# Spreading a softmax maximum with float32r matmuls instead of float32 ones, in a Perceiver kernel on one Trainium2 core

## The chip, the cores and the metric

The kernel runs on one core of a Trainium2 chip. A core has five engines that run side by side and meet only at semaphores: TensorE (PE, with its weight loads listed as PEld), VectorE (DVE), ScalarE (ACT), GpSimd (POOL) and SyncE (SP), which here issues all transfers. The metric is the device time of one execution in microseconds (us). Before the change it is 2708.26 us, the median of three runs that lie between 2706.93 and 2709.93 us.

## What is computed

The reference is a small Perceiver with six residual blocks, on an input `x` of 8 batches of 64 rows by 512 and a context of 8 batches of 1601 rows by 512. Each block is fed a layer-normalised `x`:

```
x = x + cross_attention_0(ln(x), ctx, Wq, bq, Wkv, bkv, Wo, bo)   # 32 query heads of 128, 8 key/value heads
x = x + state_space_block(ln(x), ...)                             # 1024 channels, 16 states, a scan over 64 steps
x = x + ternary_linear(ln(x), weight, bias)
x = x + cross_attention_1(ln(x), ctx)                             # no weights
x = x + causal_self_attention(ln(x), wq, wk, wv, wo)              # 32 heads of 16, rotary
x = x + octonion_ffn(ln(x), w_gate, w_up, w_down)
```

The change is in the first block, whose core is, for every batch and key/value head:

```
scores = einsum('blkgd,bmkd->bkglm', q, k) * scale
attn   = softmax(scores, axis=-1)          # over the 1601 context rows
o      = einsum('bkglm,bmkd->blkgd', attn, v)
out    = o @ Wo + bo
```

A softmax is unchanged when the same number is taken off all scores of a query, so the number taken off need not be the exact maximum, as long as it is the same in numerator and denominator.

## The kernel before

**Units.** The first attention is cut into 64 units, one for each batch `b` and key/value head `i`. A unit has 256 queries (four heads of 64 rows) and 1601 context rows, in 13 tiles of up to 128. Scores are held transposed: context rows on the 128 partitions, the 256 queries along the free axis. `x_k` (L354) makes keys, `x_v` (L319) values, `x_s` (L369) the scores, `x_av` (L454) the product with the values, `x_o` (L466) the normalisation, and `x_wo` (L496) the output projection. Keys, values and scores (and from batch 2 on the output projection) are made of three float32r products of a high and a low part (`split`, L100: ACT rounds the high part, DVE or POOL makes the low part); the product with the values and the sum over ones (L472) are plain float32.

**The maximum.** `x_s` keeps a running maximum `mx` on DVE (L390, L392, L395), which leaves a maximum for each partition and query. `x_max` (L397) turns it with two transposes on PE into `m_ps` (L403), and one DVE reduction (L405) writes the negative maximum of each query to the two columns of `mc`. `x_spread` (L408) puts that number on all partitions: for each half `h` of 128 queries a matmul (L412) has as stationary operand column `h` of `mc`, broadcast to 128 by 128, and as moving operand the identity; entry (p, j) of its result is the negative maximum of query j. `x_exp` (L416) then adds this to the score tiles `S` on DVE (L426), takes the exponential on ACT (L427) and sums on POOL (L429, L446, L448, L452).

**Order of the work.** `x_all` (L527) goes through the units in six steps each. While unit n makes its scores, unit n-1 goes through maximum, spread, exponential and value product, so that one unit of each kind is in flight. `x_spread` is emitted in step 0, after the unit's first score tiles. Beside this run side programs: `prep` (L616, splits of weights), and `chain` (L779), the five later blocks, for four groups of two batches. `advance` (L1331, in `run`) emits pieces of them after every piece of the first attention, by fixed costs (X_COST, PREP_COST, CHAIN_COST) that the change leaves alone. The fourth group's chain starts after the last unit, so its work and what is left of the third group's form the tail. The calls only give a first order: the tile framework's scheduler then puts the instructions of each engine in an order of its own, by times that it estimates. Only the DVE, ACT and POOL instructions of the side programs are kept in program order, while the first attention runs (`Late`, L55). So the price that the scheduler sees for one matmul can move others.

**Constants.** `consts` (L147) makes the identity `ident` on POOL (L152) at the start.

Of the kernel before, what the change touches and what calls it, by code (L numbers as in the profile page):

```python
# [9 lines left out]
FR = mybir.dt.float32r  # L10
# [6 lines left out]
P = 128  # L17
# [61 lines left out]
class Kernel:  # L79
# [67 lines left out]
    def consts(self):  # L147
        nc, i = self.nc, self.i
        c = self.ctx.enter_context(self.tc.tile_pool(name="const", bufs=1))
        self.c = c  # L150
        self.ident = c.tile([P, P], FP, name="ident")
        make_identity(nc, self.ident)  # L152
        self.eps5 = c.tile([P, 1], FP, name="eps5")
        nc.gpsimd.memset(self.eps5, 1e-5)
        self.ones = c.tile([P, P], FP, name="ones")
        nc.gpsimd.memset(self.ones, 1.0)
        self.eps6 = c.tile([P, 1], FP, name="eps6")
        nc.gpsimd.memset(self.eps6, 1e-6)

        def ld(name, shape):  # L160
            t = c.tile(shape, FP, name="c_" + name)
            nc.sync.dma_start(out=t, in_=i[name])
            return t

        self.bq = ld("bq", [P, 32])
        self.bk = ld("bk", [P, NKV])
        self.bv = ld("bv", [P, NKV])
# [229 lines left out]
    def x_max(self, b, i):  # L397

        nc = self.nc
        m = self.mf.pop((b, i))  # L400
        ps = self.px.tile([P, 2, 256], FP, name=self.nm("m_ps"), tag="m", bufs=MB)
        for h in range(2):
            nc.tensor.transpose(ps[:, 0, h * P : (h + 1) * P], m[:, 0, h * P : (h + 1) * P], self.ident)  # L403
        col = self.sb("mc", [P, 2], pool=self.xp, bufs=2)
        nc.vector.tensor_reduce(col, ps[:, 0].rearrange("p (h k) -> p h k", k=P), AX.X, ALU.max, negate=True)  # L405
        self.mm[(b, i)] = (ps, col)

    def x_spread(self, b, i):  # L408

        ps, col = self.mm[(b, i)]  # L410
        for h in range(2):
            self.nc.tensor.matmul(  # L412
                ps[:, 1, h * P : (h + 1) * P], lhsT=col[:, h : h + 1].to_broadcast([P, P]), rhs=self.ident, start=True, stop=True
            )

    def x_exp(self, b, i, n):  # L416
# [1086 lines left out]
```

## Time and profile before

| | |
|---|---|
| median of three runs | 2708.26 us |
| the profiled execution: own time / span of its instructions | 2710.54 / 2708.8 us |
| busy share of PE, PEld, DVE, ACT, POOL | 95, 84, 62, 50, 46 % |
| mean granted TensorE clock | 0.977 |
| last spread matmul (L412) ends | about 2384 us |
| spread matmuls (L412): records, mean of one | 256, 283 ns |
| DVE additions of the maximum (L426) | 448 |

The profile lists every matmul record with its own duration, from start to end; neighbours overlap, so the pace of a run of matmuls is read from start to start or from a run's length, not from one record's duration. A float32 matmul stands as two records, each with a weight load; a float32r matmul as one. The 64 units have two halves, so the 256 records of L412 are 128 matmuls. "Idle before" is the time in which the engine had nothing to run before an instruction, with the instruction that ended it. Lines such as L65 are helpers' lines through which the side programs are recorded.

### The profile page before, as it was taken

The page shows a single profiled execution, that of the slowest core. Times are in us where ns is not written, and L with a number is a line of the kernel's source. Part 1 is how long each engine was busy: PE and PEld are TensorE (multiplying, and loading weights), DVE is VectorE, ACT ScalarE, POOL GpSimd, SP SyncE. Part 2 cuts the span into 40 slices and gives each one's busy share as a digit, 9 for nine tenths or more (in the row PEclk, how much of TensorE's full clock was granted, in tenths as well). Part 3 has the DMA queues.
Part 4 walks back from the last instruction along what each step waited for, and adds up shares of the span by engine and source line. Part 5 has one row for each costly group of instructions (what it writes and reads, how often), then busy time and mean ns, then how long its engine had stood idle before and what let it go on. Part 6 is the DMA issues. An engine that isn't in the chain of part 4 may idle for free.

```text
span 2708.8 us, 43887 instructions
## 1 busy us (share of the span) xinstructions
PE 2569.9 (95%) x16288; PEld 2274.8 (84%) x16288; DVE 1670.9 (62%) x2723; ACT 1354.6 (50%) x3128; POOL 1253.5 (46%) x1243
## 2 busy tenths in 40 slices
PE   7999999999999899999999999999999999977787
PEld 6999999889899799978988988988898888964545
DVE  4444345577687865545577676554657777668744
ACT  4444554444566554544455545544546545446443
POOL 3212434464589864422358457521239556405410
PEclk9999999999999999999999999999999999987898
DMA  9544446665666235655234543665343454476764
GB/s 309 153 141 155 137 144 227 200 209 179 212 215 204 71 117 164 210 185 172 88 110 135 157 148 101 206 197 173 101 133 91 137 162 151 141 236 216 233 234 174
DMA packets 302934, 455.59 MB, mean 168 GB/s; under 512 B 80248, under 2 KB 179576, under 8 KB 298240
## 3 DMA queue, kind: packets, MB, share of 16 engines
q1 hardware_dynamic: 302720, 452.79, 52.2%
q8 instruction: 128, 2.10, 0.3%
q14 instruction: 86, 0.70, 0.1%
HBM read 380.23 MB, written 72.48 MB: 167 GB/s over the span
## 4 chain that ended last, share of the span: by engine, by line
PE 67%; DVE 10%; POOL 9%; DMA 7%; issue 4%; ACT 3%; SPq 0%; POOLq 0%; DVEq 0%; ACTq 0%
PE v_ps L334 15%; PE k_ps L363 15%; PE o_ps L464 10%; PE s_ps L385 8%; POOL a L65 4%; DVE a L65 3%; PE w_ps L521 3%; PE acc L274 3%; PE acc L819 2%; PE acc L1095 2%; POOL ss L452 2%; PE acc L1039 2%; PE acc L774 1%; PE acc L777 1%; DMA d_wo<-b 1%
## 5 line engine op out<-in xcount | busy, mean ns | idle before, releaser
L363 PE MATMUL k_ps<-cxb,wk 128*128 128x384 f32 x2304 | 469.9, 347 | 32.1 <-DVE mx L392 16.8
L334 PE MATMUL v_ps<-wv,cxb 128*128 128x256 f32 x3456 | 471.0, 283 | 1.4 <-DVE mx L392 1.2
L334 PEld LDWEIGHTS v_ps<-wv,cxb 128*128 128x128 f32 x3456 | 439.2, 189 | 22.0 <-issue 14.0
L363 PEld LDWEIGHTS k_ps<-cxb,wk 128*128 128x128 f32 x2304 | 405.2, 191 | 50.2 <-DVE mx L392 19.8
L464 PE MATMUL o_ps<-S,v 128*128 128x256 f32 (+1 forms) x1664 | 413.3, 381 | 6.0 <-DVE rw L479 3.9
L385 PE MATMUL s_ps<-q,kt 128*128 128x256 f32 (+1 forms) x2496 | 413.7, 299 | 5.2 <-DVE kt L109 3.1
L388 ACT COPY S<-s_ps 128x512 f32<-128x512 f32 (+1 forms) x448 | 242.4, 553 | 250.0 <-PE s_ps L385 246.9
L385 PEld LDWEIGHTS s_ps<-q,kt 128*128 128x128 f32 (+1 forms) x2496 | 342.1, 185 | 28.0 <-issue 6.9
L452 POOL TENSOR_TENSOR ss<-ss,S 128x512 f32<-128x512 f32 x254 | 353.7, 1392 | 14.6 <-ACT S L427 1.5
L429 POOL TENSOR_TENSOR ss<-S,S 128x512 f32<-128x512 f32 x64 | 85.0, 1328 | 586.9 <-ACT S L427 586.6
L392 DVE TENSOR_TENSOR mx<-s_ps,mx 128x512 f32<-128x512 f32 x256 | 175.4, 685 | 289.5 <-ACT S L388 288.8
L464 PEld LDWEIGHTS o_ps<-S,v 128*128 128x128 f32 (+1 forms) x1664 | 299.5, 190 | 45.0 <-issue 5.7
L108 ACT ACTIVATE kt<-k_ps,c_bk 128x384 fp32r<-128x384 f32 (+1 forms) x256 | 152.0, 594 | 240.7 <-PE k_ps L363 239.6
L426 DVE TENSOR_TENSOR S<-S,m_ps 128x512 f32<-128x512 f32 (+1 forms) x448 | 257.3, 641 | 24.4 <-PE m_ps L412 23.9
L427 ACT ACTIVATE S<-S 128x512 f32<-128x512 f32 (+1 forms) x448 | 247.4, 599 | 44.4 <-DVE S L426 43.8
L109 DVE SCALAR_TENSOR_TENSOR kt<-k_ps,c_bk,kt 128x384 fp32r<-128x384 f32 (+1 forms) x256 | 161.0, 629 | 170.9 <-ACT kt L108 169.4
L337 ACT COPY v<-v_ps 128x256 f32<-128x256 f32 (+1 forms) x416 | 152.7, 369 | 198.1 <-PE v_ps L334 195.7
L334 PE MATMUL v_ps<-wv,cxt 128*128 128x256 f32 (+1 forms) x1536 | 213.2, 286 | 2.7 <-DVE kt L109 1.6
L334 PEld LDWEIGHTS v_ps<-wv,cxt 128*128 128x128 f32 (+1 forms) x1536 | 195.3, 176 | 15.5 <-issue 6.5
L65 DVE TENSOR_TENSOR_SCAN a<-a,a 128x512 f32<-128x512 f32 x96 | 156.1, 1629 | 65.4 <-POOL a L65 65.4
L363 PE MATMUL k_ps<-cxt,wk 128*128 128x450 f32 x768 | 181.1, 378 | 0.9 <-DVE mx L392 0.8
L65 ACT ACTIVATE a<-lv,c_A_log 128x128 f32<-128x128 f32 x384 | 123.0, 394 | 105.3 <-DVE a L65 103.8
(358 smaller groups left out, 3971.3 us busy)
## 6 DMA issues: line engine op xcount, KB each, us to landing
wo<-d_wo SPq DMA_DIRECT2D x96, 512.0 KB, 5.0
wk<-d_wk SPq DMA_DIRECT2D x63, 512.0 KB, 3.8
wv<-d_wv SPq DMA_DIRECT2D x31, 1024.0 KB, 5.6
cst<-in_ctxT_dram SPq DMA_DIRECT2D x96, 192.0 KB, 3.1
b<-in_ctxN_dram SPq DMA_DIRECT2D x36, 512.0 KB, 3.9
d_q<-q_t SPq DMA_DIRECT2D x32, 512.0 KB, 4.4
q<-d_q SPq DMA_DIRECT2D x64, 256.0 KB, 3.5
d_wo<-b SPq DMA_DIRECT2D x32, 512.0 KB, 3.1
```

The costliest lines, as they stand in the source:

```text
L65: return lambda *a, **k: self.tc.keep_in_program_order(f(*a, **k))
L109: eng.scalar_tensor_tensor(lo, src, bias, hi.bitcast(FP), ALU.add, ALU.subtract)
L334: nc.tensor.matmul(ps[:r], lhsT=cx[:, a, c, o : o + r], rhs=w[:, m, c, :], start=k == 0, stop=k == 11)
L337: nc.scalar.copy(vt[:r], ps[:r])
L363: nc.tensor.matmul(ps[:, :wd], lhsT=w[:, a, c, :], rhs=cx[:, m, c, :], start=k == 0, stop=k == 11)
L385: nc.tensor.matmul(sp[:r, gi, :], lhsT=kt[:, a, o : o + r], rhs=q[:, m, :], start=k == 0, stop=k == 2)
L388: nc.scalar.copy(s[:r, :n], sp[:r, :n])
L392: nc.vector.tensor_tensor(mx, sp, S[0] if len(S) == 1 else mx, ALU.max)
L426: nc.vector.tensor_tensor(sv, sv, ps[:r, 1:2].to_broadcast([r, w, 256]), ALU.add)
L427: nc.scalar.activation(sv, sv, AF.Exp, scale=ISC)
L452: nc.gpsimd.tensor_tensor(ss, ss, S[n], ALU.add)
L464: nc.tensor.matmul(ps[:, 0], lhsT=self.v[(b, j, t)][:r, hc : hc + P], rhs=S[t // 2][:r, t % 2], start=t == 0, stop=t == NT - 1)
```

## The change

The column tile `mc` gets the type float32r, so the DVE reduction at L405 rounds the negative maximum when it writes it. A second identity, `ident_r`, is made once in `consts` by an ACT copy that writes float32r. The two spread matmuls of a unit take these two as operands, so both operands are float32r. Shapes, the number of calls and the places where they are called stay as they are. All exponentials and sums of a query use the same rounded maximum.

```diff
@@ consts
         self.ones = c.tile([P, P], FP, name="ones")
         nc.gpsimd.memset(self.ones, 1.0)
+        self.ident_r = c.tile([P, P], FR, name="ident_r")
+        nc.scalar.copy(self.ident_r, self.ident)
         self.eps6 = c.tile([P, 1], FP, name="eps6")
@@ x_max
-        col = self.sb("mc", [P, 2], pool=self.xp, bufs=2)
+        col = self.sb("mc", [P, 2], FR, pool=self.xp, bufs=2)
         nc.vector.tensor_reduce(col, ps[:, 0].rearrange("p (h k) -> p h k", k=P), AX.X, ALU.max, negate=True)
@@ x_spread
             self.nc.tensor.matmul(
-                ps[:, 1, h * P : (h + 1) * P], lhsT=col[:, h : h + 1].to_broadcast([P, P]), rhs=self.ident, start=True, stop=True
+                ps[:, 1, h * P : (h + 1) * P], lhsT=col[:, h : h + 1].to_broadcast([P, P]), rhs=self.ident_r, start=True, stop=True
             )
```

## The prediction

> **What bounds the kernel now.** I read the page first (busy shares, then the slices), then the busy time of the engines by stretch of the span, since a mean over stages hides who is the bound in each.
>
> ```profile
> span 2708.8 us, 43887 instructions
> PE 2569.9 (95%) x16288; PEld 2274.8 (84%) x16288; DVE 1670.9 (62%) x2723; ACT 1354.6 (50%) x3128; POOL 1253.5 (46%) x1243
> ...
> PE   7999999999999899999999999999999999977787
> ...
> DVE  4444345577687865545577676554657777668744
> ```
>
> ```profile
> core 0: us, PE busy (x) PEld busy (x) DVE busy (x) ACT busy (x) POOL busy (x), PEclk, DMA share, GB/s
> ...
> 400.00:800.00 400.00, 389.06 (x2509) 358.15 (x2508) 275.60 (x470) 201.20 (x439) 220.17 (x208) 0.99 0.63 202
> 800.00:1200.00 400.00, 383.17 (x2500) 354.30 (x2499) 250.88 (x367) 210.72 (x504) 241.10 (x240) 0.99 0.52 162
> 1200.00:1600.00 400.00, 398.01 (x2631) 357.51 (x2630) 259.53 (x426) 208.71 (x484) 187.36 (x187) 1.00 0.43 135
> ...
> 2395.00:2709.00 314.00, 249.34 (x1344) 160.41 (x1344) 198.69 (x378) 142.16 (x377) 89.28 (x97) 0.86 0.67 223
> ```
>
> PE is the bound until about 2395 us: it is busy 383 to 398 of every 400 us, and no other engine comes near. What is taken from PE there should come off the time, except where PE then waits for another engine: 10.9 idle us in the first stretch shown, 16.8 in the second, 2.0 in the third. The last 314 us, the tail, are another matter: PE is busy 79% at a granted clock of 0.86, and chains of dependent work set the pace.
>
> The spread is on this bound. The PE timeline around the first unit's spread:
>
> ```profile
> 84.11 0.84 PE L334 MATMUL v_ps<-wv,cxb 128*128 128x256 f32 x6
> 84.79 0.60 PE L412 MATMUL m_ps<-ident,mc 128*128 128x128 f32 x4
> 85.15 0.96 PE L334 MATMUL v_ps<-wv,cxb 128*128 128x256 f32 x6
> ```
>
> The first row ends at 84.95 us, the second at 85.39: the four float32 records push the value matmuls back by 0.44 us, 111 ns a record. Over 64 units that is 28 us of PE time, and the change can win no more than a part of it.
>
> **The change part by part.**
>
> *The spread matmuls.* They go from four records a unit to two. What one float32r record with 128 moving columns costs, no row shows: every float32r matmul of the trace moves 256 columns or more. Two things limit a record, its stream and its weight load. The chain of waits gives streams, the groups of weight loads give loads:
>
> ```profile
> 70.73 2.09 PE k_ps L363 x12
> 72.82 1.37 PE v_ps L334 x12
> ```
>
> ```profile
> L334 PEld LDWEIGHTS v_ps<-wv,cxb 128*128 128x128 f32 x3456 | 439.2, 189 | 22.0 <-issue 14.0 <-DVE mx L392 1.6 <-DVE kt L109 0.6
> L334 PEld LDWEIGHTS v_ps<-wv,cxt 128*65 128x65 f32 x384 | 46.3, 137 | 3.8 <-issue 1.4 <-DVE mx L392 1.3
> L412 PEld LDWEIGHTS m_ps<-ident,mc 128*128 128x128 f32 x256 | 35.6, 193 | 10.6 <-DVE mc L405 7.3 <-issue 2.2 <-DVE b L65 0.2
> L403 PEld LDWEIGHTS m_ps<-ident,mx 128*128 128x128 f32 x128 | 16.5, 140 | 3.4 <-DVE mx L395 1.1 <-issue 0.8
> ```
>
> Streams: 384 columns take 2.09/12 = 174 ns, 256 take 1.37/12 = 114, so 128 would take 114 - 60 = 54 ns. Loads, float32r too: 128 stationary columns take 189 ns, 65 take 137, so a column costs 52/63 = 0.83 ns, and 128 columns 106 ns beside a fixed part that overlaps. A 256-column stream (114 ns) hides a load of 106; a 128-column stream of 54 cannot. The loads of a broadcast column already went at 111 ns a record in the spread before. I take 111 ns: the removed thing is then half of the records at an unchanged pace, 2 x 111 = 222 ns a unit, 64 x 0.222 = 14.2 us. Ends: with the stream as the limit, 444 - 108 = 336 ns a unit, 21.5 us. With a record as slow as the slowest float32r one of the trace, 512 columns at 230 ns, 2 x 230 = 460 replaces 444, a loss of 1.0 us. I stay with 14.2, since load rows of the same type and width carry it.
>
> The Trainium skill says in "TensorE: Matmul & The Clock Gate", section "LDWEIGHTS (loading the stationary operand)", that a load takes its column count over 1.2 in ns, whatever the rows: 107 ns for 128 columns, which agrees with the 106 above and speaks against a gain by the stream. Its section "Back-to-back issue gap" gives 56 ns for an isolated matmul of 128 columns. The sum would be 64 x (444 - 214) = 14.7 us by the first and 64 x (444 - 112) = 21.2 by the second; no row of this case has a plain matmul whose stream is shorter than its load, so the trace does not yet decide.
>
> *What of it reaches the end.* Where PE next waits for DVE or ACT, an earlier PE gains nothing. The stretches with over 10 us of PE idle time (400 to 1200, 1600 to 2000, 2200 to 2395) hold 1395 of the 2335 us after the start, so between none and 60% could be lost. Their idle time is only 4% of them (52 us), so most units inside run back to back; I take a sixth: 14.2 x 5/6 = 11.8 us.
>
> *What waits around it.* The DVE addition L426 waits for the spread, 23.9 us in 22 cases; it gets its maximum 0.2 us earlier, and exponentials and sums behind it too, off the bound. The spread itself waits for the reduction L405 in some units (PE idle 5.9 us); that stays, and what is late next there is again `mc`.
>
> *The reduction's new type.* 64 times 424 ns before, two columns out. DVE writes float32r elsewhere without a visible price (L109, 128x384, 629 ns, against L392, 128x512 in float32, 685). Its spread of 389 to 426 ns bounds it: at most 64 x 0.04 = 2.4 us either way, off the bound except in those 5.9 us. I take nothing.
>
> *The second identity.* One ACT copy of 128x128, under the 0.50 us that the 128x384 cast takes. `ident` is ready at 1.5 us and ACT idles 6.49 us until the first weights land at 8.50; the copy stands ahead of that cast. Without that cover it would be 0.5 us, once.
>
> *The order.* The built program has the same matmuls, transfers and DVE and POOL instructions, and one more on ACT, but in another order. Up to the 31st spread the PE order is nearly the same; from there to the last one up to 41 fewer matmuls of the side programs lie before a given spread. SP's 1331 transfers shift by up to 24 places, POOL's instructions by up to 31. After the last spread lie 36 more matmuls than before, 14 more DVE and 11 more ACT instructions, all but one on each of PE and DVE from the third group's state-space block: 16 float32 matmuls of L819 (32 records x 111 ns = 3.6 us) and 20 of 512 columns (20 x 0.23 = 4.6), 8.2 us of PE. They leave the time before the tail and enter it. PE has 65 idle us in the tail. Ends: all 8.2 us vanish there, a gain; or they sit on the chain that ends last, the loss worked out below. PE's sum is unchanged, and I take nothing.
>
> Sum: -11.8 us. The profiled execution took 2710.5 us, 1.7 more than its span and 2.2 more than the median of the three runs. From 2710.5 the sum gives 2698.7, from the median 2696.5; I predict against the median. A difference under 0.2% (5.4 us) can't be told from no change here.
>
> **The rivals.**
>
> *The stream is the limit.* 21.5 x 5/6 = 17.9 us, 2690.4; with the 8.2 us vanishing in the tail, 2682.2. For it: transposes of 128 columns load in 140 ns, so a 128-column load can be shorter. Against: they are another mode, and the float32r loads stand at 189. Chance 0.20.
>
> *The gain is absorbed, or the matmul is no faster.* PE's waits for DVE in the busy stretches grow by what PE saves, or a narrow float32r matmul runs at the float32 pace. Time 2703 to 2709. For it: DVE at 69% from 400 to 800, and no row for the new form. Against: PE's 398 of 400 from 1200 to 1600. Chance 0.18.
>
> *The third group's chain ends last (slower).* In the profile before, the state-space matmuls that now stand behind the last spread begin at 2352 us, 31 us ahead of that spread's 2383. If the third group's later blocks run back to back and end last, they slip by up to 31 us against the spread, while the spread comes 14.2 + 8.2 = 22 us earlier: +9 us, 2717. It decides as soon as the tail after the last spread grows by more than 22 us. For it: the chain of waits passes from 2445 to 2475 through the third group's second cross-attention. Against: from 2480 to 2540 it runs through L956, a scan that only the fourth group has, which starts earlier by those 22 us. Chance 0.20.
>
> **How the numbers follow.** The forecast, 2696.5, has 0.42. Faster than by 0.2% are the forecast and the stream case, 0.62; the same is the absorbed case, 0.18; slower the third, 0.20. The range goes from the stream case with its tail, 2682, to just under the slow case, 2716.
>
> **What would show it.** L412 has 128 records instead of 256, and a spread pushes its neighbours back by about 0.22 us (0.11 if the stream limits, 0.44 if nothing is won). Its weight loads stay near 190 ns. The last L412 ends near 2362 us instead of 2384 (14.2 + 8.2 earlier), and the tail after it is as long as now or up to 10 us longer. PE busy drops by some 14 us, DVE, ACT and POOL stay within a few us. I am wrong if the last spread is not earlier by at least 10 us, or if the tail grows by more than the lead.

## The result and the profile after

The changed kernel takes 2730.45 us (median of four runs, 2728.46 to 2733.72); the kernel before, measured beside it, takes 2707.6 us (four runs, 2703.51 to 2709.93). The ratio is 1.0087, with a 95% interval of 1.007 to 1.0105: slower, and outside the predicted range. The profiled execution took 2728.46 us, its span 2726.6 us, 17.8 us more than the span before. One of the four executions of e1 below, the profiled one, ran at a lower clock and took 3597 us; it is left out of e1's time, and e1 has no row of its own in the trace table.

All lines of the changed kernel below L157 are two higher than before: the spread is L414, its reduction L407, the state-space projection L821. The head of its page, with the slices of PE and DVE:

```profile
span 2726.6 us, 43661 instructions
...
PE 2564.1 (94%) x16160; PEld 2260.4 (83%) x16160; DVE 1672.8 (61%) x2723; ACT 1351.5 (50%) x3129; POOL 1243.1 (46%) x1243
...
PE   7999999999999899999999999999999999866787
...
DVE  4444445667687765545658677643658767648635
```

PE has 128 records fewer and is busy 5.8 us less, and still the span is longer: PE is idle 23.6 us more. The busy time by stretch says where (columns: stretch, its length, then busy us and instruction count of PE, PEld, DVE, ACT and POOL, granted clock, DMA share, GB/s):

```profile
400.00:800.00 400.00, 386.88 (x2493) 355.15 (x2493) 272.47 (x469) 200.69 (x439) 222.17 (x208) 0.99 0.62 204
800.00:1200.00 400.00, 383.33 (x2485) 355.53 (x2483) 255.18 (x373) 211.78 (x507) 237.09 (x239) 0.98 0.49 160
1200.00:1600.00 400.00, 398.26 (x2621) 357.21 (x2620) 256.39 (x417) 208.06 (x482) 182.10 (x185) 1.00 0.43 138
2200.00:2395.00 195.00, 171.52 (x1029) 153.91 (x1028) 131.36 (x183) 91.08 (x227) 97.04 (x104) 0.96 0.43 141
2395.00:2726.00 331.00, 254.72 (x1344) 160.92 (x1344) 200.77 (x382) 143.17 (x380) 90.23 (x97) 0.83 0.64 215
```

The first three stretches are as full as before. The stretch from 2200 to 2395 us is not: before it reads

```profile
2200.00:2395.00 195.00, 182.20 (x1139) 166.82 (x1137) 133.96 (x195) 94.63 (x234) 98.50 (x105) 0.98 0.48 153
```

so 10.7 idle us more have come in there, 5.0 of them after 2364 us, behind the changed kernel's last spread, and 11.6 more in the tail (76.3 against 64.7).

The spread itself did what was forecast. The PE timeline of the changed kernel around the first unit's spread, and its groups of `m_ps`:

```profile
84.64 0.84 PE L336 MATMUL v_ps<-wv,cxb 128*128 128x256 f32 x6
85.32 0.33 PE L414 MATMUL m_ps<-ident_r,mc 128*128 128x128 f32 x2
85.49 0.93 PE L336 MATMUL v_ps<-wv,cxb 128*128 128x256 f32 x6
```

```profile
L414 PEld LDWEIGHTS m_ps<-ident_r,mc x128: 185/188/333, 85.2 to 2363.2; 128*128 128x128 f32 x128
L414 PE MATMUL m_ps<-ident_r,mc x128: 218/274/624, 85.3 to 2363.4; 128*128 128x128 f32 x128
L407 DVE TENSOR_REDUCE mc<-m_ps x64: 392/424/427, 82.0 to 2362.6; 128x2 fp32r<-128x256 f32 x64
```

From the end of the value matmuls ahead (85.48 us) to the end of those behind (86.42) are 0.94 us; before the change it was 1.16 (84.95 to 86.11). The two float32r records save 0.22 us a unit; over all spreads the medians of the same two stretches are 0.94 and 1.16 us too. Weight loads have a median of 188 ns (190 before) and the reduction one of 424, as before. The last spread ends at 2363.8 us instead of 2384.0, 20.2 us earlier.

Behind it, time is lost. The DVE timeline of the changed kernel (start, duration, instruction; in brackets the idle time before it and what ended it):

```profile
2390.72 0.69 DVE L526 TENSOR_TENSOR x<-w_ps,x 128x512 f32<-128x512 f32 x1 [9.28 <-PE w_ps L523]
...
2411.59 0.69 DVE L65 TENSOR_TENSOR xr<-acc,x 128x512 f32<-128x512 f32 x1 [11.16 <-PE acc L779]
2412.20 0.68 DVE L141 BATCH_NORM_STATS2 ln_st<-x 128x6 f32<-128x512 f32 x1
```

The first row completes the fourth group's input. The second ends the third group's state-space block. The third is the first instruction of the fourth group's chain: it starts 20.8 us after its input. Before, the three stood in another order:

```profile
2394.24 0.69 DVE L65 TENSOR_TENSOR xr<-acc,x 128x512 f32<-128x512 f32 x1 [1.40 <-PE acc L777]
...
2404.33 0.69 DVE L524 TENSOR_TENSOR x<-w_ps,x 128x512 f32<-128x512 f32 x1 [1.21 <-PE w_ps L521]
2405.06 0.69 DVE L141 BATCH_NORM_STATS2 ln_st<-x 128x6 f32<-128x512 f32 x1
```

So the last spread ends 20.2 us earlier and the fourth group's input is ready 13.6 us earlier (2391.4 against 2405.0), but the third group's state-space block ends 17.4 us later, and by then nothing hides it. The PE timeline of the changed kernel shows it standing alone on PE, waiting for its own activations and weight transfers:

```profile
2399.54 0.79 PE L776 MATMUL acc<-w,a 128*128 128x512 f32 x1 [6.09 <-ACT a L65]
...
2403.42 0.80 PE L778 MATMUL acc<-w,a 128*128 128x512 f32 x1 [1.80 <-DMA w<-d_wout]
...
2410.33 0.80 PE L778 MATMUL acc<-w,a 128*128 128x512 f32 x1 [1.65 <-DMA w<-d_wout]
...
2415.75 1.08 PE L729 MATMUL acc<-ident,a 128*128 128x128 f32 x4 [4.20 <-DVE a L144]
```

What ends last is told by tile names: the third group's later blocks use tiles with an `_r` at the end once the tail has begun (L97). PE and DVE at the end of the changed kernel:

```profile
2719.99 0.75 DVE L1299 SCALAR_TENSOR_TENSOR xr<-acc,s_oct,xr 128x512 f32<-128x512 f32 x1 [1.00 <-PE acc L779]
...
2722.47 0.40 PE L779 MATMUL acc<-w_r,b_r 128*128 128x512 f32 x1
2722.90 0.75 DVE L1299 SCALAR_TENSOR_TENSOR xr<-acc,s_oct,xr 128x512 f32<-128x512 f32 x1 [1.52 <-PE acc L779]
```

The last product is `w_r,b_r`, the third group's. Before, the third group's was done five microseconds ahead of the end and the fourth's came last:

```profile
2699.50 0.39 PE L777 MATMUL acc<-w_r,b_r 128*128 128x512 f32 x1
...
2704.62 0.40 PE L777 MATMUL acc<-w,b 128*128 128x512 f32 x1
```

### The profile page after: what moved, and what is told of

The parts are those of the page before. It is cut to its first block, busy times and chain, and to the rows that moved or that the text cites. A ratio compares the mean times of both kernels' runs of the same rounds, so it can differ in the third digit from the quotient of the medians.

```text
span 2726.6 us, 43661 instructions
## 1 busy us (share of the span) xinstructions
PE 2564.1 (94%) x16160; PEld 2260.4 (83%) x16160; DVE 1672.8 (61%) x2723; ACT 1351.5 (50%) x3129; POOL 1243.1 (46%) x1243
## 4 chain that ended last, share of the span: by engine, by line
PE 66%; POOL 9%; DVE 9%; DMA 7%; issue 5%; ACT 3%; SPq 0%; POOLq 0%; DVEq 0%; ACTq 0%
PE v_ps L336 15%; PE k_ps L365 14%; PE o_ps L466 9%; PE s_ps L387 8%; POOL a L65 4%; DVE a L65 3%; PE acc L276 3%; PE w_ps L523 2%; POOL ss L454 2%; PE acc L1097 2%; PE acc L776 2%; PE acc L1041 2%; PE acc L821 2%; PE acc L779 2%; POOL b L65 1%
## 5 line engine op out<-in xcount | busy, mean ns | idle before, releaser
L336 PEld LDWEIGHTS v_ps<-wv,cxb 128*128 128x128 f32 x3456 | 437.2, 188 | 23.9 <-issue 13.1
L365 PEld LDWEIGHTS k_ps<-cxb,wk 128*128 128x128 f32 x2304 | 403.1, 190 | 48.9 <-DVE mx L394 17.4
```

The costliest lines, as they stand in the source:

```text
L336: nc.tensor.matmul(ps[:r], lhsT=cx[:, a, c, o : o + r], rhs=w[:, m, c, :], start=k == 0, stop=k == 11)
L365: nc.tensor.matmul(ps[:, :wd], lhsT=w[:, a, c, :], rhs=cx[:, m, c, :], start=k == 0, stop=k == 11)
```

## The experiments

Theories. A: the float32r spread is cheaper and the time would have fallen; what costs is the other order that the scheduler made, with the third group's state-space block late. B: the new type itself costs, somewhere that the first reading missed. Within A there are two ways to lose: A1, the late block holds the start of the fourth group; A2, the late block makes the third group's own chain end last. The expectations name mainly A1, which was the theory of the first eight runs.

For all kernels the same points were read from the traces. "Block" is the end of the third group's last state-space output matmul (`acc<-w,a`), "ready" the end of the last L524 (L526 in the changed line numbers), "start" the fourth group's first L141, and the outputs are the issues of the last two output transfers, given to their groups by the tile names of the last products ahead of them. All in us; a row is one profiled execution, the ratio, with its 95% interval, comes from several executions of each kernel.

| kernel | spread, order | block | ready | start | third out | fourth out | ratio to before |
|---|---|---|---|---|---|---|---|
| before | float32, its own | 2394.2 | 2405.0 | 2405.1 | 2700.7 | 2705.8 | 1 |
| changed | float32r, its own | 2411.6 | 2391.4 | 2412.2 | 2723.7 | 2720.8 | 1.0087 (1.007 to 1.0105) |
| e1 | float32r, as before | - | - | - | - | - | 0.9953 (0.9936 to 0.997) |
| e8 | float32r, as before | 2394.6 | 2405.4 | 2405.4 | 2701.2 | 2706.3 | 0.997 (0.996 to 0.998) |
| e2 | float32, as changed | 2424.2 | 2402.9 | 2424.9 | 2735.3 | 2732.4 | 1.0111 (1.0094 to 1.0128) |
| e3 | float32, SPAN 2.7 | 2403.6 | 2403.1 | 2404.2 | 2705.8 | 2710.9 | 0.9997 (0.9987 to 1.0008) |
| e4 | float32, SPAN 2.5 | 2379.7 | 2410.3 | 2410.3 | 2689.5 | 2703.3 | 0.9978 (0.9967 to 0.9988) |
| e6 | float32, SPAN 2.9 | 2425.0 | 2399.4 | 2425.7 | 2721.9 | 2727.0 | 1.0065 (1.0048 to 1.0082) |
| e5 | float32r, as e4 | 2370.6 | 2400.7 | 2400.8 | 2680.5 | 2694.3 | 0.9932 (0.9914 to 0.9951) |
| e10 | float32r, order of float32 at SPAN 2.75 | 2371.1 | 2397.1 | 2397.2 | 2689.5 | 2694.6 | 0.997 (0.9955 to 0.9984) |
| e7 | float32r, its own at SPAN 2.5 | 2390.8 | 2390.6 | 2391.4 | 2707.3 | 2675.4 | 1.0006 (0.9995 to 1.0016) |
| e9 | changed, residual on ACT and POOL | 2401.4 | 2387.0 | 2401.4 | 2711.2 | 2708.3 | 1.0011 (1.0 to 1.0023) |
| e11 | changed, two tail pools | 2429.8 | 2396.6 | 2396.7 | 2734.9 | 2693.6 | 1.0076 (1.0058 to 1.0094) |
| e12 | before, two tail pools | 2395.5 | 2407.0 | 2407.0 | 2702.3 | 2707.5 | 0.9996 (0.9987 to 1.0006) |

### The type without the order, and the order without the type

In e1, e5, e8 and e10 the scheduler sees float32 operands; when the program is complete, the operands of the 128 spread matmuls are exchanged for float32r views of the same tiles. In e2 it is the other way round. So the order of every engine stays that of the type that the scheduler saw (plus the one ACT copy of the identity where the float32 kernel has none). In all five `mc` is written as float32r, as in the change.

```diff
@@ x_spread (e1, e5, e8, e10)
-    lhsT=col[:, h : h + 1].to_broadcast([P, P]), rhs=self.ident
+    lhsT=col.bitcast(FP)[:, h : h + 1].to_broadcast([P, P]), rhs=self.ident_r.bitcast(FP)
@@ kernel, when the program is complete (e2 with float32)
+    for blk in nc.cur_f.blocks:
+        for k, i in enumerate(blk.instructions):
+            if i.opcode == "Matmult" and any(str(x.memref).startswith("ident_r") for x in i.ins):
+                args = [PhysicalAccessPattern(..., dtype=float32r, ...) for x in i.ins]
+                blk.instructions[k] = copy.replace(i, ins=args)
```

> Every instruction stands where it stood before the change (and the one ACT copy at the start); only the 128 spread matmuls are float32r. If the order made the loss: a spread costs 222 ns less, 64 x 0.222 = 14.2 us of PE, and the tail after the last spread stays at 325 us as before, so 2691 to 2697. If the narrow float32r matmul, the rounded maximum or the second identity makes the loss: 2725 to 2735, as the change.

> The kernel of the first run once more (order of before, float32r spread matmuls): for a profile at the full clock. 0.993 to 0.997 of before; a spread pushes its neighbours back by 222 ns less than before; the last spread comes 10 to 14 us earlier than 2384; the tail behind it stays within 3 us of before's 325.

> Every instruction stands where it stands after the change, but the spread matmuls read the same two tiles as float32. If the order made the loss: slower than the change by up to 14 us, 2730 to 2745, and the tail after the last spread stays above 345 us. If the float32r matmul made it: 2705 to 2712, as before.

Measured: e1 has a median of 2697.66 us (three executions), e8, the same kernel on another chip, 2702.89; the kernel before takes 2712.82 and 2712.68 beside them. With the order kept, the new type gains 0.3 to 0.5%, 8 to 13 us. e2 takes 2740.79: the new order with the old type loses 1.1%, 28 us, and the changed kernel is about the sum of the two. B has fallen. The profiled execution of e8 was the slowest of its ten (2711.03 us), so e8's row in the table is no picture of its median. In it the spread saves its 0.22 us and the tail is as long as before (324.7 us), but the last spread ends at 2384.5 us and not 10 to 14 us earlier than before, as was expected. The pairs of runs with one order show that lead: the last spread ends at 2363.8 us in the changed kernel against 2373.2 in e2, and at 2375.0 in e5 (below) against 2384.6 in e4. So 9.4 us of the changed kernel's 20.2 belong to the type, and the rest to its order.

### How late the third group may be, without the new type

The constant `SPAN[2]` sets when the third group's pieces are due; 2.6 in both kernels.

```diff
-SPAN = [3.1,3.1,2.6,0.2]
+SPAN = [3.1,3.1,2.7,0.2]     # e3; 2.5 in e4, 2.9 in e6
```

> The kernel before with one number changed, the third group's planned length, 2.7 for 2.6. Float32 spread as before. In its order 12 matmuls of the third group's state-space output stand behind the last spread (5 before, 24 after the change), and that block's residual addition stands on DVE behind the last attention addition, ahead of the fourth group's first statistics. If work of the third group behind the last spread makes the loss: slower than before by 5 to 15 us, 2713 to 2723. If the type does: 2705 to 2712.

> The kernel before with the third group's planned length at 2.5. None of that block's matmuls stands behind the last spread, and its residual addition is 39 DVE instructions ahead of the last attention addition. If work of the third group behind the last spread makes the loss: not slower than before, 2695 to 2710. If the tail does not depend on it: no relation, anything from 2700 to 2720.

> The kernel before, float32 spread, with the third group's planned length at 2.9. Its order has 24 matmuls of the third group's state-space output and 24 of its gate projection behind the last spread, and the block's residual addition 10 DVE instructions behind the last attention addition, ahead of the fourth group's first statistics: as the change has it (24, 16 and 10). If that place makes the loss: the fourth group's first statistics wait 15 to 25 us for the residual, and the time is 2728 to 2745 beside a before of 2713. If the loss belongs to the new matmul or to another part of the new order: 2705 to 2720.

Measured: e3 2712.51, e4 2706.29, e6 2729.7 us. e4 lies within both of its cases and decides nothing alone. The loss looked for in e3 did not come: 12 output matmuls of the block stand behind its last spread, but the block ends at 2403.6 us, together with the fourth group's input (2403.1), and so holds nothing. In e6 it ends 25.6 us after the input and the time rises by 0.65%, with the float32 spread. The DVE timeline of e6 has the pattern of the changed kernel, and its last product on PE is `w,b`, the fourth group's:

```profile
2398.67 0.69 DVE L524 TENSOR_TENSOR x<-w_ps,x 128x512 f32<-128x512 f32 x1 [8.42 <-PE w_ps L521]
...
2425.08 0.69 DVE L65 TENSOR_TENSOR xr<-acc,x 128x512 f32<-128x512 f32 x1 [13.35 <-PE acc L777]
2425.69 0.68 DVE L141 BATCH_NORM_STATS2 ln_st<-x 128x6 f32<-128x512 f32 x1
```

```profile
2725.81 0.40 PE L777 MATMUL acc<-w,b 128*128 128x512 f32 x1
```

So the loss needs no new type; it needs a late block. In e6 the group that ends last is the fourth, held at its start (A1); the third is done 5.1 us ahead of it.

### The new type with the block early

e5 is e4's order with the float32r spread, e10 the order of a float32 kernel with `SPAN[2]` 2.75 with it, both by the exchange above. e7 is the changed kernel with `SPAN[2]` 2.5, in the order that the scheduler then makes.

> The order of the kernel before with the third group's planned length at 2.5, unchanged, with float32r spread matmuls put in its places. If the gain of a spread is 14.2 us wherever the order is kept: 14 us under that order's own time (2706 beside a before of 2713), so 0.9915 to 0.994 of before. If the order takes what the matmul gives whatever the order is: 0.997 to 1.000.

> The order that the scheduler makes with float32 spread matmuls and SPAN[2] = 2.75 (third group's pieces due later, yet no output matmul of it behind the last spread and its residual 34 DVE instructions ahead of the fourth group's statistics), with the spread matmuls then put to float32r. If what counts is only where the third group's state-space block stands against the fourth group's start, this does as well as the order of SPAN[2] = 2.5 with float32r: L141 within 2 us of its input and 2692 to 2702. If the value of SPAN itself matters (a later due time costs by the later blocks of the third group), the time is 2705 to 2720.

> The changed kernel with the third group's planned length at 2.5 and an order of its own. 12 matmuls of the third group's state-space output and none of its gate projection stand behind the last spread, the residual directly behind the last attention addition. If the place of that block makes the loss: the fourth group waits under 3 us, and the time is 2695 to 2708 beside a before of 2713. If not: near the change, 2725 to 2735.

Measured: e5 2695.89 us against 2712.68 before, the best kernel of the study; e10 2702.31 against 2711.43, 0.3 us above the first case; e7 2713.68. In e5 and e10 the block ends at 2371 us, about when the last spread does. In e5 the order's gain and the matmul's add up: its ratio lies 0.0046 below e4's, 12.5 us, for the type alone (the two were run on different chips, and their intervals together leave some 6 us either way, an estimate). e10 has no float32 run of its order beside it. That e10 is faster than before with a due time later than the original 2.6 speaks against the due time itself as the cause, and for the place where the scheduler puts the block. The row of e10's block, 25 us ahead of the fourth group's start:

```profile
2371.17 0.69 DVE L65 TENSOR_TENSOR xr<-acc,x 128x512 f32<-128x512 f32 x1 [1.64 <-PE acc L777]
...
2396.43 0.69 DVE L524 TENSOR_TENSOR x<-w_ps,x 128x512 f32<-128x512 f32 x1 [3.46 <-PE w_ps L521]
2397.15 0.69 DVE L141 BATCH_NORM_STATS2 ln_st<-x 128x6 f32<-128x512 f32 x1
```

e7 was a part miss, and the first sign of A2: its fourth group starts without a wait, at 2391.4 us, and is done at 2675.4, 30 us earlier than before. But the third group is not done until 2707.3, and the time is that of before.

### What holds the fourth group

e9 takes the third group's residual off DVE, so that L141 no longer stands behind it there (the residuals of the first two groups go the same way).

```diff
@@ mamba
-        nc.vector.tensor_tensor(xo, wps, x, ALU.add)
+        if tail: nc.vector.tensor_tensor(xo, wps, x, ALU.add)
+        else: nc.scalar.copy(xo, wps); nc.gpsimd.tensor_tensor(xo, xo, x, ALU.add)
```

> The changed kernel, but the residual addition after the state-space block of the first three groups is an ACT copy and a POOL addition instead of one DVE addition. So on DVE the fourth group's first statistics (L141) no longer stand behind the third group's residual; on PE the third group's last 12 output matmuls still stand between the last projection matmul of the first attention and the fourth group's transposes. In the changed kernel L141 waited 20 us after the fourth group's input was ready (2391.4, 2411.6). If DVE's queue alone held the fourth group, L141 starts within 2 us of its input, the transposes within 10 us of it, and the time falls by 10 to 20 us, to 2710 to 2720. If PE's queue holds it too, L141 is early, but the transposes (L729) still come only after the third group's last output matmul, near 2411, and the time stays within 5 us of the changed kernel's, 2725 to 2735.

Measured: 2715.1 us. Neither case fits: the time fell as if DVE's queue had been the holder, but L141 was not early. Its row in the DVE timeline:

```profile
2401.41 0.69 DVE L141 BATCH_NORM_STATS2 ln_st<-x 128x6 f32<-128x512 f32 x1 [12.55 <-PE acc L779]
```

With no residual ahead of it, L141 still waited 12.55 us for the third group's last output matmul, of which it reads nothing. The explanation that e11 tests is memory. When the last unit is done, the kernel closes the pools of the first attention and of the side programs' state-space blocks, and opens one pool for the tail over both (L1367 to L1370 of the changed kernel):

```python
                    xctx.close()
                    actx.close()
                    self.pc = ctx.enter_context(tc.tile_pool(name="pt", bufs=3, space=PSUM))
                    self.ca = self.cp = self.tp = ctx.enter_context(tc.tile_pool(name="tp", bufs=2))
```

By this the first tile of the tail, the one that L141 writes, waits until the third group's block has given up its memory, whatever the queues look like. e9's time goes with its block, which ended 10 us earlier: both outputs came 12.5 us earlier than in the changed kernel. e11 tests the pool: the tiles that the fourth group uses first get a pool over the attention's memory alone, opened before `actx` is closed; six later kinds of tiles get a second one. e12 does the same to the kernel before.

```diff
@@ sb
-            if tag in REST and self.tp and not self.tail:
+            if self.tail and tag in LATE_TAGS: pool = self.pl
+            elif tag in REST and self.tp and not self.tail: ...
@@ run
                     xctx.close()
-                    actx.close()
                     self.pc = ...
                     self.ca = self.cp = self.tp = ctx.enter_context(tc.tile_pool(name="tp", bufs=2))
+                    actx.close(); self.pl = ctx.enter_context(tc.tile_pool(name="tl", bufs=2))
@@
+LATE_TAGS = ("b2", "b4", "kb", "s1m", "s1s", "a1m")
```

> The changed kernel, with the tail's memory in two pools instead of one: the tiles that the fourth group uses first lie in a pool over the memory of the first attention alone, and only six later kinds of tiles in a second pool over the memory that the third group's state-space block gives back. All work is the same. If the fourth group's first statistics (L141) are held because the tail's one pool opens only when the third group's state-space block has given its memory back, they start here within 2 us of their input (2391 in the changed kernel, where they started at 2412), and the time falls by 10 to 30 us, to 2697 to 2717. If the third group's own chain is what ends last (the rival of the prediction), L141 is early as well, but the time stays at 2722 to 2735.

> The same two tail pools on the kernel before (float32 spread). There the third group's state-space block ends at 2394 us and the fourth group's input is ready at 2405, so that the one pool held nothing: L141 starts with its input as before, and the time is the same within 5 us, 2704 to 2714. If the two pools are worth something by themselves (another order in the tail), the time falls by 10 us or more here too, and a gain of the changed kernel from them proves nothing about the wait.

Measured: e11 2733.26 us against 2711.99 before; e12 2711.71. The DVE timeline of e11:

```profile
2395.94 0.69 DVE L526 TENSOR_TENSOR x<-w_ps,x 128x512 f32<-128x512 f32 x1 [9.98 <-PE w_ps L523]
2396.67 0.69 DVE L141 BATCH_NORM_STATS2 ln_st<-x 128x6 f32<-128x512 f32 x1
...
2429.83 0.69 DVE L65 TENSOR_TENSOR xr<-acc,x 128x512 f32<-128x512 f32 x1 [0.32 <-PE acc L779]
```

The wait is gone, so the pool was what held the fourth group; and the time has not fallen (the second case of the expectation), so freeing the fourth group's start is not enough. At the end of e11 the fourth group's last DVE instruction stands 41 us ahead of the third's:

```profile
2692.85 0.75 DVE L1299 SCALAR_TENSOR_TENSOR xr<-acc,s_oct,xr 128x512 f32<-128x512 f32 x1 [5.74 <-PE acc L779]
...
2734.08 0.75 DVE L1299 SCALAR_TENSOR_TENSOR xr<-acc,s_oct,xr 128x512 f32<-128x512 f32 x1 [2.59 <-PE acc L779]
```

The freed fourth group's matmuls (L821, `acc<-a,w`, 64 records from 2401.7 us on) went in between those of the third group's block, which now ends at 2429.8 us instead of 2411.6, and the third group ends last. That is A2, in an order that is not the changed kernel's. In the changed kernel both ways are at work: its third group ends last, at 2723.7, but its fourth, held at its start, is done only 2.9 us before that, 15.0 us later than before the change. No run frees the fourth group's start and keeps the block's end at 2411.6, so how much each way costs alone was not measured.

### What the table says together

From the end of its block to its output, the third group takes 297 to 318 us in all thirteen rows that have them (median 310). The fourth takes 284 to 309 from its start (median 301), and with one tail pool its start is the later of "ready" and "block". Where the block ends well before the input is ready (before, e4, e5, e8, e10, e12), the fourth group ends last, 293 to 301 us after the input. Where it ends at the input or later, the last output comes 302 to 317 us after the block's end, whichever group's it is: the third's in the changed kernel, e2, e7, e9 and e11, the fourth's in e3 and e6. An earlier attention then gains nothing. The changed kernel is the second kind: 2411.6 + 312.1 = 2723.7.

## Why the prediction was wrong

- **The spread matmuls**: right. 222 ns a unit were to be saved; 0.22 us was measured from the quoted rows. The stream case, which would have saved 0.34 us, fell. The Trainium skill, "TensorE: Matmul & The Clock Gate", section "LDWEIGHTS (loading the stationary operand)", has 107 ns for a load of 128 columns; the 111 ns a record before the change and the 0.22 us saved by two records fewer agree. Its 56 ns for an isolated matmul ("Back-to-back issue gap") leaves out the load, as that section says itself, and so does not describe these matmuls, each of which has a load of its own; its figure for pairs of load and matmul, about 81 ns, was not met here either.
- **What reaches the end**: right in size, for a kept order. 11.8 us were taken; 8 and 13 us (e8, e1) and 12.5 (e5 against e4) were measured. These are too far apart to test the sixth that was taken off.
- **What waits around it, the reduction's type, the identity**: right, nothing to be seen. The reduction has a median of 424 ns in its new type (the two rows compared for it differ in operation and width and said little), and the waits for `mc` around the tile `m_ps` went from 13.1 to 7.3 us.
- **"The order. ... PE's sum is unchanged, and I take nothing"**: this step failed. The working had counted what moves behind the last spread and priced it at 8.2 us of PE. Its price is not its PE time. It is the 17.4 us by which the block ends later, because what follows it, about 310 us of the third group's later blocks, can't start earlier and is about as long as the whole tail; and the fourth group, held by the block's memory, ends 15.0 us later as well. e2 measures the order at +1.1%.
- **The slower rival**, "the third group's chain ends last", was right, though it had only 0.20. Its point of decision held: the tail after the last spread grew by 38.0 us (324.8 to 362.8), more than 22. Its size was too small. It gave the block a slip of up to 31 us against the spread and a lead of 22; measured were 37.6 (from 10.2 us after the spread to 47.8) and 20.2, so +17.4 instead of +9. With the third group's own chain 5.6 us longer, and less the 5.1 us by which the fourth came last before, which the rival's sum left out, this makes 17.9 us, the difference between the last outputs.
- **The argument against that rival** failed through a tie that the profile before doesn't show: the fourth group's scan L956 was to start 22 us earlier, but it started 7 us later (2472.6 against 2465.7), as L141 did (2412.2 against 2405.1), because the tail's one pool waits for the third group's block. Before the change the pool was free 11 us ahead of the input, and the tie cost nothing.
- **PE busy** fell by 5.8 us instead of 14: by 11.2 up to 2395 us, while the tail, at a granted clock of 0.83 instead of 0.86, got 5.4 more. Between runs with one order it fell by 10.0 (e8 against before; the changed kernel against e2) and 15.3 us (e5 against e4).

What stays open is why a cheaper spread makes the scheduler put the block later. It was seen at every `SPAN[2]` that was run with the float32r price (2.6 and 2.5: block 47.8 and 25 us after the last spread), and the float32 price gave both early and late blocks (2.75: early; 2.7: 26.0 us after the last spread; 2.9: 51 us), but the rule by which it chose was not traced.

## What to carry to other kernels

When a scheduler orders the program by its own prices, a cheaper instruction is two changes: the saving and a new order. Building the order with the old price and exchanging the instruction afterwards measures them apart (here -0.3 to -0.5% and +1.1%), and may keep the gain. In the order's difference, look not at how much work moved but at when the block that ends there is finished and how long the chain behind it is; and look which memory a late block still holds, since a pool that opens over it ties chains together that share no data.

## What was not expected of the hardware

The gain of the shorter matmul isn't all in its own record. In the first unit the two float32r records end 0.17 us after the value matmul ahead of them, less than two loads at 111 ns, and the six value matmuls behind them end 0.77 us after the spread instead of 0.72 before, 0.05 us later. Only the stretch from neighbour to neighbour shows the 0.22 us.

Where PE idles more, its granted clock is lower in these rows. From 2395 to 2420 us, where up to 2411.6 the third group's block stands alone, the changed kernel's PE is busy 11.09 us at a granted clock of 0.52, the kernel before 18.29 us at 0.80:

```profile
2395.00:2420.00 25.00, 11.09 (x32) 7.30 (x33) 8.13 (x22) 4.23 (x14) 1.48 (x5) 0.52 0.47 166
2420.00:2500.00 80.00, 53.93 (x295) 39.73 (x294) 63.67 (x131) 45.67 (x137) 28.68 (x33) 0.67 0.67 227
```

```profile
2395.00:2420.00 25.00, 18.29 (x93) 15.31 (x95) 14.33 (x41) 9.16 (x28) 1.79 (x8) 0.80 0.80 275
2420.00:2500.00 80.00, 59.94 (x354) 39.38 (x350) 64.72 (x126) 46.40 (x140) 33.31 (x35) 0.77 0.76 244
```

The Trainium skill describes this in "TensorE: Matmul & The Clock Gate", section "HAM oscillation — how this bites in real kernels": gaps of PE from waits for transfers throttle the matmuls that follow them. The rows agree, though the longest gap here, 6.09 us, was ended by ACT; what part of the 17.8 us the lower clock made up was not measured.
